# State space layer of a decoder: norm, D term and copies on ScalarE, the dt chain on operands in PSUM, the update of x two turns behind its power

## The chip, the cores and the metric

One core of a Trainium2 chip runs the whole kernel in one launch. The metric is the device time of one execution in microseconds (us), as the median of several runs. Engines are named as in the profile: PE (TensorE matmul; PEld its weight loads), DVE (VectorE), ACT (ScalarE), POOL (GpSimd), SP (SyncE, which issues DMAs). PSUM is the memory that PE writes, SBUF the other one on the chip.

## The reference

A decoder of two layers on x of 64 sequences x 128 positions x 256 features, all in float32. It has six blocks, each added to x: a state space layer (Mamba-like), cross attention, a recurrence, self attention, a wide cross attention, and a mixture of experts. Only the first block is touched by the change:

```
x = x + ssm(_layernorm(x))

zxbcdt = einsum('bld,ed->ble', x, in_proj_w)          # z 512, xBC 768, dt 8
xBC = silu(causal_conv4(xBC) + conv_b)                # x_part 512, B 128, C 128
dt = softplus(dt + dt_bias);  A = -exp(A_log)         # 8 heads
step:  decay = exp(A * dt_t)
       state = state * decay + (x_t * dt_t) outer B_t
       y_t = einsum('bhpn,bn->bhp', state, C_t)
y = y + x_part * D_full
y = y * silu(z)
y = y * rsqrt(mean(y*y) + EPS) * norm_w
return einsum('ble,de->bld', y, out_proj_w)
```

The kernel computes the scan over 128 positions as matrix products: with dA the product of dt and A, exp of its segment sums (`seg`) times B C^T (`gm`) is a 128x128 matrix `m` for each head, and y is `m` times `xdt` (x times dt).

## The kernel before

x stays in SBUF all the time, in 16 tiles `X[g]` of a group of four sequences (128 positions on the partitions, 4 x 256). The state space layer runs over the 16 groups and, in each, over four sequences; other blocks follow, one after the other, with tiles of their own.

Two generators write the layer. `mamba_inputs(g)` (L353) does a group: the norm (`norm`, L168: statistics on DVE, the root as a power on POOL at L165, then four subtract-and-multiply instructions on DVE, L191), the transposition of the normalised x on PE with a copy of one half on ACT (L204) and one on DVE (L206), then from the transposed x eight values dt a position (`pd`, L386), six convolutions (`conv`, L365) and four gates (`gate`, L379). A convolution is a projection on PE into one bank of PSUM, a scaled copy on ACT (L369), three multiply-adds on DVE (L373), a tanh on ACT (L362, which overwrites the projection's bank) and a last product on DVE (L363), which leaves `xc` in SBUF; a gate is a projection, a tanh and a product (`zs`). dt is softplus, written as max(v, 0) plus a series for log(1 + exp(-|v|)) (L390 to L407), 19 small instructions on DVE on tiles of 128x32 in SBUF, and one Exp on ACT (L392).

`mamba(g, b)` (L424) does a sequence: `ua` on POOL (L432), pg, px and seg on PE, an Exp over 128x1024 on ACT (L452), `m` on DVE (L455), py on PE (L461), the D term as four multiply-adds of 128x128 on DVE (L466), the gate and the sum of squares on POOL and ACT (L469 to L474), the output projection po (L479, with the sum of squares at L483), and the last three: ms on DVE (L488), its power on POOL (L165, `rs`), and the update of x on DVE (L490).

PSUM: the tag "mm" has six banks, which projections, pd, px, pg, py, po and the transposes take in turn; `seg` has the other two. A bank goes back when its last reader is done.

What sets the order: `run` (L49) gives each generator that is active one step a turn, from yield to yield; group g starts at turn 8g, sequence i at turn 2i + 8. This order is a priority only. A scheduler then fixes the order of each engine's queue when the kernel is built, and each engine works its queue strictly in that order, waiting on semaphores. SP's queue has in this stage the loads of x and weights and, once a sequence, a DMA that clears 1 MB of a scratch buffer (`clear`, L342), which nothing in the layer reads.

Of the kernel before, what the change touches and what calls it, by code (L numbers as in the profile page):

```python
# [7 lines left out]
F32 = mybir.dt.float32  # L8
I32 = mybir.dt.int32
AF = mybir.ActivationFunctionType  # L10
ALU = mybir.AluOpType
# [4 lines left out]
P = 128  # L16
D = 256
G = 4
T = G * P
LN_EPS = 1e-5  # L20
# [17 lines left out]
def mid(ap, n):  # L38

    return ap.unsqueeze(1).to_broadcast([ap.shape[0], n, ap.shape[1]])  # L40
# [22 lines left out]
def tile_decoder(ctx: ExitStack, tc: tile.TileContext, a: dict, out: bass.AP):  # L63
# [48 lines left out]
    X = []  # L112
# [83 lines left out]
    def transposed(work, ps, xn, bufs=2):  # L196

        xnT = [work.tile([P, T], F32, tag=f"xnT{c}", name=f"xnT{c}", bufs=bufs) for c in range(2)]
        for c in range(2):
            pt = ps.tile([P, T], F32, tag="mm", name="pt_ln")  # L200
            for b in range(G):
                nc.tensor.transpose(pt[:, b * P:(b + 1) * P], xn[:, b, c * P:(c + 1) * P], ident)  # L202
            if c == 0:
                nc.scalar.copy(xnT[c], pt)  # L204
            else:
                nc.vector.tensor_copy(xnT[c], pt)  # L206
        return xnT
# [143 lines left out]
    nc.gpsimd.tensor_scalar_mul(dpar, dpar, 0.5)  # L351

    def mamba_inputs(g, work, ps, got):  # L353
        xn = norm(work, g)
        yield
        xnT = transposed(work, ps, xn)
        yield

        def silu2(dst, u, th=None):
            if th is None:  # L360
                th = work.tile([P, T], F32, tag="th", name="th", bufs=2)
            nc.scalar.activation(th, u, AF.Tanh, scale=0.5)  # L362
            nc.vector.scalar_tensor_tensor(dst, th, 1.0, u, ALU.add, ALU.mult)  # L363

        def conv(c):  # L365
            pc = project(ps, win, 512 + c * P, P, xnT)
            acc = work.tile([P, G, P], F32, tag="acc", name="acc", bufs=2)
            pv = pc.rearrange("p (b t) -> p b t", b=G)
            nc.scalar.activation(  # L369
                acc, pv, AF.Identity, bias=convb[:, c:c + 1], scale=convw[:, c, 3:4]  # L370
            )
            for k in range(1, 4):
                nc.vector.scalar_tensor_tensor(  # L373
                    acc[:, :, k:], pv[:, :, :P - k], convw[:, c, 3 - k:4 - k], acc[:, :, k:],
                    ALU.mult, ALU.add,
                )
            silu2(xc[:, c, :], acc.rearrange("p b t -> p (b t)"), pc)

        def gate(c):  # L379
            silu2(zs[:, c, :], project(ps, win, c * P, P, xnT))  # L380


        pd = ps.tile([P, T], F32, tag="mm", name="pd")
        pdv = pd[:, :G * 8].rearrange("p (b h) -> p b h", b=G)
        for b in range(G):
            project_rows(pdv[:, b, :], xnT, win, b, slice(1280, 1288))  # L386
        v, u, r, s2, q, dt, da = (
            work.tile([P, G, 8], F32, tag=f"dt_{i}", name=f"dt_{i}", bufs=2) for i in range(7)
        )
        nc.vector.tensor_tensor(v, pdv, mid(dtb, G), ALU.add)  # L390
        nc.vector.scalar_tensor_tensor(u, v, -1.0, v, ALU.mult, ALU.max)
        nc.scalar.activation(u, u, AF.Exp, scale=-1.0)  # L392
        xc = work.tile([P, 6, T], F32, tag="xc", name="xc", bufs=2)
        conv(4)
        yield
        nc.vector.tensor_scalar(r, u, 2.0, None, ALU.add)
        nc.vector.reciprocal(r, r)
        nc.vector.tensor_tensor(u, u, r, ALU.mult)
        nc.vector.tensor_tensor(s2, u, u, ALU.mult)
        nc.vector.tensor_scalar(q, s2, 1.0 / 17, None, ALU.mult)  # L400
        for n in (15, 13, 11, 9, 7, 5, 3):
            nc.vector.scalar_tensor_tensor(q, q, 1.0 / n, s2, ALU.add, ALU.mult)
        nc.vector.scalar_tensor_tensor(q, q, 1.0, u, ALU.add, ALU.mult)
        nc.vector.tensor_scalar(v, v, 0.0, None, ALU.max)
        nc.vector.scalar_tensor_tensor(dt, q, 2.0, v, ALU.mult, ALU.add)
        nc.vector.tensor_tensor(da, dt, mid(negA, G), ALU.mult)  # L406
        nc.vector.tensor_scalar(dt, dt, 0.5, None, ALU.mult)  # L407
        conv(5)
        yield
        conv(0)  # L410
        conv(1)
        yield
        conv(2)
        zs = work.tile([P, 4, T], F32, tag="zs", name="zs", bufs=2)
        gate(0)
        yield
        conv(3)
        gate(1)
        yield
        gate(2)  # L420
        gate(3)
        got[g] = xc, zs, dt, da

    def mamba(g, b, work, ps, got):  # L424
        xc, zs, dt, da = got[g]
        clear(g * G + b)
        if g * G + b == B - 1:
            clear(B)
        tb = slice(b * P, (b + 1) * P)

        ua = work.tile([P, 8, P], F32, tag="ua", name="ua", bufs=2)
        nc.gpsimd.tensor_tensor(out=ua, in0=mid(upper, 8), in1=last(da[:, b, :], P), op=ALU.mult)  # L432

        pg = ps.tile([P, T], F32, tag="mm", name="pg")
        nc.tensor.matmul(pg[:, :P], lhsT=xc[:, 4, tb], rhs=xc[:, 5, tb], start=True, stop=True)
        gm = work.tile([P, P], F32, tag="gm", name="gm", bufs=2)
        nc.vector.scalar_tensor_tensor(gm, pg[:, :P], 0.25, upper, ALU.mult, ALU.mult)
        px = ps.tile([P, T], F32, tag="mm", name="px")
        for j in range(4):
            nc.tensor.transpose(px[:, j * P:(j + 1) * P], xc[:, j, tb], ident)  # L440
        xdt = work.tile([P, 8, 64], F32, tag="xdt", name="xdt", bufs=3)
        nc.vector.tensor_tensor(
            xdt, px.rearrange("p (h e) -> p h e", h=8), last(dt[:, b, :], 64), ALU.mult
        )
        yield
        seg = ps.tile([P, 8, P], F32, tag="seg", name="seg")
        for hf in range(2):
            nc.tensor.matmul(
                seg[:, hf * 4:hf * 4 + 4, :], lhsT=lower, rhs=ua[:, hf * 4:hf * 4 + 4, :],
                start=True, stop=True,  # L450
            )
        nc.scalar.activation(seg, seg, AF.Exp)  # L452
        yield
        m = work.tile([P, 8, P], F32, tag="m", name="m", bufs=3)
        nc.vector.tensor_tensor(m, seg, mid(gm, 8), ALU.mult)  # L455
        yield
        yield
        py = ps.tile([P, 4, P], F32, tag="mm", name="py")
        for h in range(8):
            r0 = (h % 2) * 64  # L460
            nc.tensor.matmul(  # L461
                py[r0:r0 + 64, h // 2, :], lhsT=xdt[:, h, :], rhs=m[:, h, :], start=True, stop=True
            )
        y = work.tile([P, 4, P], F32, tag="y", name="y", bufs=2)
        for j in range(4):
            nc.vector.scalar_tensor_tensor(  # L466
                y[:, j, :], xc[:, j, tb], dpar[:, j:j + 1], py[:, j, :], ALU.mult, ALU.add
            )
        nc.gpsimd.tensor_tensor(out=y, in0=y, in1=zs[:, :, tb], op=ALU.mult)  # L469
        ysq = work.tile([P, 4, P], F32, tag="ysq", name="ysq")  # L470
        nc.scalar.activation(ysq, y, AF.Square)
        nc.gpsimd.tensor_tensor(out=ysq[:, 0:2], in0=ysq[:, 0:2], in1=ysq[:, 2:4], op=ALU.add)
        sq = work.tile([P, P], F32, tag="sq", name="sq", bufs=3)
        nc.gpsimd.tensor_tensor(out=sq, in0=ysq[:, 0], in1=ysq[:, 1], op=ALU.add)  # L474
        yield
        yield
        po = ps.tile([P, T], F32, tag="mm", name="po")
        for j in range(4):
            nc.tensor.matmul(  # L479
                po[:, :D], lhsT=y[:, j, :], rhs=wout[:, j, :], start=(j == 0), stop=(j == 3)  # L480
            )
        yield
        nc.tensor.matmul(  # L483
            po[:, D:D + 1], lhsT=sq, rhs=ones[:, 0:1], start=True, stop=True
        )

        ms = work.tile([P, 1], F32, tag="ms", name="ms", bufs=2)
        nc.vector.tensor_scalar(ms, po[:, D:D + 1], 1.0 / 512, 4 * LN_EPS, ALU.mult, ALU.add)  # L488
        rs = power(work, "rs", ms)
        nc.vector.scalar_tensor_tensor(  # L490
            X[g][:, b, :], po[:, :D], rs, X[g][:, b, :], ALU.mult, ALU.add
        )

    with phase_pool("work1", "left") as work, phase_pool("ps1", space=PSUM) as psp:
        ps = PsumPool(psp, {"mm": 6, "seg": 1})
        got = {}
        run(
            [(8 * g, mamba_inputs(g, work, ps, got)) for g in range(NG)]
            + [(2 * i + 8, mamba(i // G, i % G, work, ps, got)) for i in range(B)]
        )  # L500
    w1_cm.__exit__(None, None, None)

# [740 lines left out]
```

## Time and profile before

| what | us |
|---|---|
| median of three runs | 3499.11 (3480.84 to 3499.29) |
| profiled execution, its own time | 3451.55 |
| its span, first to last instruction | 3449.8 |
| of it the state space layer, up to the last update of x | 789 |

The profiled execution is one run, some 1.4% below the median of the others. Inside the first 789 us the engines are busy so:

```profile
0.00:789.00 789.00, 711.03 (x3328) 425.20 (x3328) 683.22 (x1555) 280.42 (x418) 337.64 (x351) 0.97 0.32 105
789.00:1811.00 1022.00, 983.53 (x6174) 614.16 (x6174) 572.31 (x1204) 595.62 (x2387) 353.90 (x301) 0.99 0.05 17
```

A line gives the stretch and its length, then the busy time of PE, PEld, DVE, ACT and POOL with the number of instructions, the mean granted clock of PE (1 is full), the mean share of the DMA engines and GB/s. The second line is what follows, mainly cross attention and the recurrence. A line of instructions, as the prediction shows them, has the source line, engine, operation, the tiles written and read, the count, then busy us and mean ns of one, then the idle time of the engine just before them and what ended it.

### The profile page before, as it was taken

What the parts mean: (1) busy time and instruction counts of PE and PEld (TensorE: products, weight loads), DVE (VectorE), ACT (ScalarE), POOL (GpSimd) and SP (SyncE); (2) the same over time, 40 slices, a digit from 0 to 9 for tenths busy, and PEclk for the clock granted to TensorE, in tenths of its full rate; (3) what the DMA queues carried; (4) which work ended last, traced back from release to release, by engine and by line L of the source; (5) the groups of instructions that cost most, each with busy time, mean ns of one, the idle gap of its engine ahead of it and who ended that gap; (6) DMA issues with size and microseconds to landing.
All of it is one profiled execution on the core that took longest, in us unless ns stands there. A gap on an engine that the chain in (4) does not pass through costs nothing. (4 is left out here: it accounts for less than half of the span.)

```text
span 3449.8 us, 51423 instructions
## 1 busy us (share of the span) xinstructions
PE 3186.7 (92%) x17998; PEld 2011.8 (58%) x17998; DVE 2211.8 (64%) x5354; ACT 1627.1 (47%) x5829; POOL 1237.1 (36%) x1156
## 2 busy tenths in 40 slices
PE   7899899997999999999999788999999999689989
PEld 4555555554566666666656544555656565468845
DVE  7989899974555565556554375676676767543355
ACT  3333333333655565556655255565656666213300
POOL 3444344446233223332231055232322222223277
PEclk9999999998999999999999888998999999789999
DMA  9980000001000000000000111010101111157655
GB/s 313 343 290 1 1 1 1 1 14 30 13 13 13 25 13 13 13 24 14 13 13 13 34 44 56 30 45 25 44 32 41 35 39 36 62 175 228 201 183 178
DMA packets 172978, 229.65 MB, mean 67 GB/s; under 512 B 19760, under 2 KB 143152, under 8 KB 172720
## 3 DMA queue, kind: packets, MB, share of 16 engines
q1 hardware_dynamic: 154752, 180.19, 16.2%
q0 software_dynamic: 17968, 46.18, 4.3%
q8 instruction: 142, 2.33, 0.3%
q14 instruction: 116, 0.95, 0.1%
HBM read 113.71 MB, written 127.93 MB: 70 GB/s over the span
## 5 line engine op out<-in xcount | busy, mean ns | idle before, releaser
L267 ACT ACTIVATE e<-s,mx 128x128 f32<-128x128 f32 x2048 | 721.1, 378 | 398.2 <-DVE mx L256 247.4
L333 POOL TENSOR_TENSOR kbd<-kT,consts 128x512 f32<-128x512 f32 x192 | 201.6, 1050 | 863.2 <-PE s L247 861.9
L267 ACT ACTIVATION_READ_ACCUMULATOR e<-s,mx 128x1 f32 x2048 | 444.8, 217 | 0.0
L247 PE MATMUL s<-kbd,qT 64*128 64x512 f32 x1024 | 369.5, 657 | 5.4 <-ACT e L267 3.8
L216 PE MATMUL proj<-xnT,win 128*128 128x512 f32 x640 | 312.8, 629 | 48.5 <-DVE xc L363 45.0
L278 PE MATMUL pt<-consts,e 128*128 128x128 f32 x2048 | 326.7, 286 | 25.0 <-ACT e L267 18.6
L278 PEld LDWEIGHTS pt<-consts,e 128*128 128x128 f32 x2048 | 235.9, 143 | 131.8 <-ACT e L267 65.2
L282 DVE COPY eT<-pt 128x512 f32<-128x512 f32 x256 | 175.6, 686 | 157.1 <-PE pt L278 155.2
L216 PEld LDWEIGHTS proj<-xnT,win 128*128 128x128 f32 x640 | 121.7, 200 | 195.2 <-issue 117.2
L873 POOL DMA_INDIRECT xs<-xnr,r_rows x128 | 125.5, 981 | 269.7 <-DMA xs<-xnr,r_rows 188.4
L373 DVE SCALAR_TENSOR_TENSOR acc<-proj,convw,acc 128x508 f32<-128x508 f32 (+2 forms) x288 | 209.5, 731 | 9.5 <-ACT acc L369 7.9
L632 PE MATMUL pu<-c,fu 128*128 128x128 f32 x1536 | 188.3, 281 | 14.9 <-DVE c L647 14.9
L309 PE MATMUL av<-eT,v 128*32 128x128 f32 x4096 | 181.5, 284 | 17.9 <-DVE oT L318 12.8
L632 PEld LDWEIGHTS pu<-c,fu 128*128 128x128 f32 x1536 | 182.6, 196 | 21.9 <-PE pv L224 13.6
L165 POOL TENSOR_TENSOR ln_rstd<-ln_ve,neghalf 128x4 f32<-128x4 f32 x96 | 97.9, 1019 | 271.1 <-DVE ln_ve L178 249.8
L252 DVE TENSOR_REDUCE mx<-s 128x4 f32<-128x512 f32 x256 | 170.1, 677 | 29.0 <-PE s L247 28.5
L432 POOL TENSOR_TENSOR ua<-consts,dt 128x1024 f32<-128x1024 f32 x64 | 121.9, 1905 | 178.3 <-DVE dt L406 150.4
L216 PE MATMUL proj<-xnT,fx 128*128 128x512 f32 x384 | 175.0, 605 | 0.5 <-ACT xnT L204 0.5
L280 ACT COPY eT<-pt 128x512 f32<-128x512 f32 x256 | 154.4, 603 | 39.9 <-PE pt L278 35.3
L309 PEld LDWEIGHTS av<-eT,v 128*32 128x32 f32 x4096 | 102.3, 110 | 118.3 <-issue 56.6
L256 DVE TENSOR_REDUCE mx<-s 128x8 f32<-128x1024 f32 x128 | 155.9, 1218 | 22.0 <-PE s L247 21.9
L191 DVE TENSOR_SCALAR xn<-x,ln_mv,ln_rstd 128x256 f32<-128x256 f32 x256 | 129.8, 552 | 37.2 <-POOL ln_rstd L165 37.2
(269 smaller groups left out, 6460.7 us busy)
## 6 DMA issues: line engine op xcount, KB each, us to landing
xs<-zeros SPq DMA_DIRECT2D x64, 1024.0 KB, 11.2
xs<-xs SPq DMA_DIRECT2D x71, 256.0 KB, 3.4
ys<-y SPq DMA_DIRECT2D x71, 256.0 KB, 2.3
ctxT<-in_ctxT_dram SPq DMA_DIRECT2D x32, 512.0 KB, 3.8
xo<-xo SPq DMA_DIRECT2D x32, 512.0 KB, 3.5
x<-in_x_dram SPq DMA_DIRECT2D x16, 512.0 KB, 8.9
xn<-xnT SPq DMA_DIRECT2D x32, 256.0 KB, 2.0
xnT<-xn SPq DMA_DIRECT2D x16, 512.0 KB, 4.3
```

Of the source, the lines that this page charges most:

```text
L216: nc.tensor.matmul(o[:m, :], lhsT=w[:, k, m0:m0 + m], rhs=rhs[k], start=(k == 0), stop=(k == 1))
L247: nc.tensor.matmul(ss[hf], lhsT=q[rows], rhs=kb[rows, :, :], start=True, stop=True)
L252: nc.vector.tensor_reduce(mxs[i], ss[i], AX.X, ALU.min)
L256: nc.vector.tensor_reduce(mx, s, AX.X, ALU.min)
L267: nc.scalar.activation(e[h // 4][:, h % 4, :], sh[h], AF.Exp, bias=mh[h], scale=-1.0, accum_out=den[:, c * 8 + h:c * 8 + h + 1],)
L278: nc.tensor.transpose(pt[:, h, :], e[i][:, h, :], ident)
L280: nc.scalar.copy(eT[i], pt)
L282: nc.vector.tensor_copy(eT[i], pt)
L309: nc.tensor.matmul(av[j * 32:j * 32 + 32, c, :], lhsT=vh(h), rhs=eT[h // 4][:, h % 4, :], start=(odd == 0), stop=(odd == 1),)
L333: nc.gpsimd.tensor_tensor(out=kb, in0=mid(k, 4), in1=last(head, P), op=ALU.mult)
L373: nc.vector.scalar_tensor_tensor(acc[:, :, k:], pv[:, :, :P - k], convw[:, c, 3 - k:4 - k], acc[:, :, k:], ALU.mult, ALU.add,)
L632: nc.tensor.matmul(pu[:, i, :], lhsT=fu[:, k, c * P:(c + 1) * P], rhs=c2[:, k, :], start=(k == 0), stop=(k == 1),)
```

## The change

Seven edits, all in the state space layer:

1. The norm is written out in `mamba_inputs`. DVE computes only an offset, -mean x rstd, for the four sequences at once; ACT applies scale and offset. The norm and its use are one step apart.
2. Both copies of the transposed x are on ACT.
3. The dt chain keeps v, u, z, s2 and dt2 in the unused columns of pd's PSUM bank instead of SBUF tiles, so that most of its instructions have one operand in PSUM and one in SBUF. The absolute value and the square are on ACT (Abs, Square), the series is scaled so that two instructions go.
4. The D term: ACT multiplies x by D into a new tile `xd` one step after the sequence starts; DVE adds it to py in one instruction of 128x512.
5. `m` has two buffers instead of three.
6. The update of x stands two yields behind the power that it needs.
7. The steps of the convolutions and gates are cut elsewhere, and the sequences start at turn 2i + 9.

```diff
     def mamba_inputs(g, work, ps, got):
-        xn = norm(work, g)
-        yield
-        xnT = transposed(work, ps, xn)
+        x = X[g]
...
+        rstd = power(work, "ln_rstd", ve)
+        yield
+
+        off = work.tile([P, G], F32, tag="ln_off", name="ln_off", bufs=2)
+        nc.vector.scalar_tensor_tensor(off, mv[:, :, 0], -1.0, rstd, ALU.mult, ALU.mult)
+        xn = work.tile([P, G, D], F32, tag="xn", name="xn")
+        for b in range(G):
+            nc.scalar.activation(
+                xn[:, b, :], x[:, b, :], AF.Identity, bias=off[:, b:b + 1], scale=rstd[:, b:b + 1]
+            )
+        yield
...
+            nc.scalar.copy(xnT[c], pt)
         yield
...
-        pdv = pd[:, :G * 8].rearrange("p (b h) -> p b h", b=G)
+        pdv, v, u, z, s2, dt2 = (
+            pd[:, i * 32:(i + 1) * 32].rearrange("p (b h) -> p b h", b=G) for i in range(6)
+        )
...
-        v, u, r, s2, q, dt, da = (
-            work.tile([P, G, 8], F32, tag=f"dt_{i}", name=f"dt_{i}", bufs=2) for i in range(7)
+        r, q, dt, da = (
+            work.tile([P, G, 8], F32, tag=f"dt_{i}", name=f"dt_{i}", bufs=2) for i in range(4)
         )
         nc.vector.tensor_tensor(v, pdv, mid(dtb, G), ALU.add)
-        nc.vector.scalar_tensor_tensor(u, v, -1.0, v, ALU.mult, ALU.max)
+        nc.scalar.activation(u, v, AF.Abs)
         nc.scalar.activation(u, u, AF.Exp, scale=-1.0)
...
-        nc.vector.tensor_scalar(r, u, 2.0, None, ALU.add)
+        nc.vector.tensor_scalar(r, u, 0.5, 1.0, ALU.mult, ALU.add)
         nc.vector.reciprocal(r, r)
-        nc.vector.tensor_tensor(u, u, r, ALU.mult)
-        nc.vector.tensor_tensor(s2, u, u, ALU.mult)
+        nc.vector.tensor_tensor(z, u, r, ALU.mult)
+        nc.scalar.activation(s2, z, AF.Square, scale=0.5)
+        conv(5)
+        yield
         nc.vector.tensor_scalar(q, s2, 1.0 / 17, None, ALU.mult)
         for n in (15, 13, 11, 9, 7, 5, 3):
             nc.vector.scalar_tensor_tensor(q, q, 1.0 / n, s2, ALU.add, ALU.mult)
-        nc.vector.scalar_tensor_tensor(q, q, 1.0, u, ALU.add, ALU.mult)
-        nc.vector.tensor_scalar(v, v, 0.0, None, ALU.max)
-        nc.vector.scalar_tensor_tensor(dt, q, 2.0, v, ALU.mult, ALU.add)
-        nc.vector.tensor_tensor(da, dt, mid(negA, G), ALU.mult)
-        nc.vector.tensor_scalar(dt, dt, 0.5, None, ALU.mult)
-        conv(5)
-        yield
+        nc.vector.scalar_tensor_tensor(q, q, 1.0, z, ALU.add, ALU.mult)
+        nc.vector.scalar_tensor_tensor(dt2, v, 0.0, q, ALU.max, ALU.add)
+        nc.vector.tensor_tensor(da, dt2, mid(negA, G), ALU.mult)
+        nc.vector.tensor_scalar(dt, dt2, 0.5, None, ALU.mult)
         conv(0)
...
         nc.scalar.activation(seg, seg, AF.Exp)
+
+        xd = work.tile([P, 4, P], F32, tag="xd", name="xd", bufs=2)
+        for j in range(4):
+            nc.scalar.mul(xd[:, j, :], xc[:, j, tb], dpar[:, j:j + 1])
         yield
-        m = work.tile([P, 8, P], F32, tag="m", name="m", bufs=3)
+        m = work.tile([P, 8, P], F32, tag="m", name="m", bufs=2)
...
-        for j in range(4):
-            nc.vector.scalar_tensor_tensor(
-                y[:, j, :], xc[:, j, tb], dpar[:, j:j + 1], py[:, j, :], ALU.mult, ALU.add
-            )
+        nc.vector.tensor_tensor(y, py, xd, ALU.add)
...
         rs = power(work, "rs", ms)
+        yield
+        yield
         nc.vector.scalar_tensor_tensor(
             X[g][:, b, :], po[:, :D], rs, X[g][:, b, :], ALU.mult, ALU.add
         )
...
-            + [(2 * i + 8, mamba(i // G, i % G, work, ps, got)) for i in range(B)]
+            + [(2 * i + 9, mamba(i // G, i % G, work, ps, got)) for i in range(B)]
```

The built order of the blocks behind the layer is the same on PE, DVE, ACT and POOL in both programs.

More of the change, by code (lines that the diff above doesn't have):

```diff
@@ L353, in mamba_inputs @@
     def mamba_inputs(g, work, ps, got):
-        xn = norm(work, g)
-        yield
-        xnT = transposed(work, ps, xn)
+        x = X[g]
+        st = work.tile([P, G, 6], F32, tag="ln_st", name="ln_st", bufs=2)
+        mv = work.tile([P, G, 2], F32, tag="ln_mv", name="ln_mv", bufs=2)
+        for b in range(G):
+            nc.vector.bn_stats(st[:, b, :], x[:, b, :])
+        for b in range(G):
+            nc.vector.bn_aggr(mv[:, b, :], st[:, b, :])
+        ve = work.tile([P, G], F32, tag="ln_ve", name="ln_ve", bufs=2)
+        nc.vector.tensor_scalar(ve, mv[:, :, 1], LN_EPS, None, ALU.add)
+        rstd = power(work, "ln_rstd", ve)
+        yield
+        off = work.tile([P, G], F32, tag="ln_off", name="ln_off", bufs=2)
+        nc.vector.scalar_tensor_tensor(off, mv[:, :, 0], -1.0, rstd, ALU.mult, ALU.mult)
+        xn = work.tile([P, G, D], F32, tag="xn", name="xn")
+        for b in range(G):
+            nc.scalar.activation(
+                xn[:, b, :], x[:, b, :], AF.Identity, bias=off[:, b:b + 1], scale=rstd[:, b:b + 1]
+            )
+        yield
+        xnT = [work.tile([P, T], F32, tag=f"xnT{c}", name=f"xnT{c}", bufs=2) for c in range(2)]
+        for c in range(2):
+            pt = ps.tile([P, T], F32, tag="mm", name="pt_ln")
+            for b in range(G):
+                nc.tensor.transpose(pt[:, b * P:(b + 1) * P], xn[:, b, c * P:(c + 1) * P], ident)
+            nc.scalar.copy(xnT[c], pt)
         yield
@@ L402, in mamba_inputs @@
             nc.vector.scalar_tensor_tensor(q, q, 1.0 / n, s2, ALU.add, ALU.mult)
-        nc.vector.scalar_tensor_tensor(q, q, 1.0, u, ALU.add, ALU.mult)
-        nc.vector.tensor_scalar(v, v, 0.0, None, ALU.max)
-        nc.vector.scalar_tensor_tensor(dt, q, 2.0, v, ALU.mult, ALU.add)
-        nc.vector.tensor_tensor(da, dt, mid(negA, G), ALU.mult)
-        nc.vector.tensor_scalar(dt, dt, 0.5, None, ALU.mult)
-        conv(5)
+        nc.vector.scalar_tensor_tensor(q, q, 1.0, z, ALU.add, ALU.mult)
+        nc.vector.scalar_tensor_tensor(dt2, v, 0.0, q, ALU.max, ALU.add)
+        nc.vector.tensor_tensor(da, dt2, mid(negA, G), ALU.mult)
+        nc.vector.tensor_scalar(dt, dt2, 0.5, None, ALU.mult)
+        conv(0)
         yield
-        conv(0)
         conv(1)
+        conv(2)
         yield
-        conv(2)
         zs = work.tile([P, 4, T], F32, tag="zs", name="zs", bufs=2)
         gate(0)
+        conv(3)
         yield
-        conv(3)
         gate(1)
-        yield
         gate(2)
```

## The prediction

> **What bounds the kernel now.** I read the page's slices first, then windows, groups by shape, waits and one timeline, all inside the stage that the change touches.
>
> ```profile
> PE   7899899997999999999999788999999999689989
> DVE  7989899974555565556554375676676767543355
> ...
> 550.00:650.00 100.00, 91.71 (x434) 54.70 (x433) 91.63 (x197) 38.61 (x58) 44.50 (x47) 1.00 0.00 1
> ...
> L406 DVE TENSOR_TENSOR dt<-dt,negA x16: 175/180/185, 30.3 to 731.5; 128x32 f32<-128x32 f32 x16
> ```
>
> A slice is 86 us. Only in the first nine (the state space layer, last update of x at 789 us) is DVE as full as PE. In the window line (busy of PE, PEld, DVE, ACT, POOL, then the granted clock) both stand at 92%. L406 runs once per group of four sequences: 16 times, 30.3 to 731.5 us, so (731.5-30.3)/15 = 46.75 us per group. That period is what can change.
>
> ```profile
> L466 DVE SCALAR_TENSOR_TENSOR y<-xc,dpar,py 128x128 f32<-128x128 f32 x256 | 73.6, 337 | 8.1 <-PE py L461 8.1
> L191 DVE TENSOR_SCALAR xn<-x,ln_mv,ln_rstd 128x256 f32<-128x256 f32 x64 | 48.3, 802 | 3.1 <-POOL ln_rstd L165 3.1
> L490 DVE SCALAR_TENSOR_TENSOR x<-po,rs,x 128x256 f32<-128x256 f32 x62 | 29.9, 483 | 48.0 <-POOL rs L165 47.9
> L407 DVE TENSOR_SCALAR dt<-dt 128x32 f32<-128x32 f32 x16 | 23.7, 1481 | 0.0
> L402 DVE SCALAR_TENSOR_TENSOR dt<-dt,dt 128x32 f32<-128x32 f32 x112 | 19.8, 177 | 0.0
> L391 DVE SCALAR_TENSOR_TENSOR dt<-dt 128x32 f32<-128x32 f32 x16 | 15.4, 962 | 0.1
> ...
> L191 DVE TENSOR_SCALAR xn<-x,ln_mv,ln_rstd 128x256 f32<-128x256 f32 x64 | 25.1, 433 | 8.5 <-POOL ln_rstd L165 8.5
> ```
>
> Two things to see. The same L191 takes 802 ns in this stage (0 to 785 us) and 433 ns between 900 and 1500 us; L407 takes 1481 ns for 32 columns where L402 takes 177. And DVE stands 47.9/16 = 3.0 us per group waiting for POOL's power before L490. DVE is thus busy 91% and stopped by its own queue for 6% more: it sets the pace.
>
> ```profile
> PE proj L216 <- DVE xc L363: 45.0, 23, 4.8
> ...
> 362.51 9.67 PE L216 MATMUL proj<-xnT,win 128*128 128x512 f32 x16 [4.76 <-DVE xc L363]
> ...
> 412.74 5.39 PE L216 MATMUL proj<-xnT,win 128*128 128x512 f32 x12 [1.05 <-DVE y L466]
> 417.96 1.89 PE L479 MATMUL po<-wout,y 128*128 128x256 f32 x8
> 419.78 1.09 PE L461 MATMUL py<-m,xdt 128*64 128x128 f32 x16
> ```
>
> PE's waits from 60 to 740 us end on DVE: the bank of a convolution comes free only when DVE has written xc. After the idle 4.76 us, 16 projection records take 9.67 us; elsewhere 12 take 5.39, that is 0.43 each after a 0.6 us tail. So a long stop is paid twice.
>
> **PE's own need.** From such rows, start to start: proj 40 records x 0.43 = 17.2; seg 16 x 0.43 = 6.9; po 32 x 0.216 = 6.9; py 64 x 0.055 = 3.5; px, pd, pt_ln, pg 48 x 0.11 = 5.3; sums 0.5. Together 40.3 us a group, 6.4 below the period.
>
> **What the Trainium skill says.** "SBUF — State Buffer", section "Who interferes with whom": DVE and GpSimd share one port pair under an exclusive lock; a DVE tensor_scalar or copy in a two-port mode, or any DVE instruction with two SBUF inputs, can lose the whole length of a GpSimd instruction to it, and one with at most one SBUF input outside those modes does not. The trace agrees: L191 and L407 are stretched while POOL's 1.9 us L432 and 1.27 us L469 run beside them. "VectorE: DVE Perf Modes", "Why PSUM operands drop a tier": an fp32 operand in PSUM keeps an instruction out of the two-port mode; L373, with one operand in PSUM, holds 731 ns with no such spread. "ScalarE: Activation LUTs", "What ACT_TABLE_LOAD costs": 186 ns + 0.833 ns per element + 93 ns per pointer operand, 93 ns overlapped; L369 (two pointers, 512) would be 798 ns, the trace has 774. "TensorE: Matmul & The Clock Gate", "What's actually happening": idleness halves the clock; the 362 us line agrees.
>
> **The change, part by part (per group, before its period is recomputed).**
> Norm: four L191, 4 x 802 = 3.2 us, leave DVE; one tiny instruction for the offset (0.2) comes, -3.0. ACT gains 4 x about 0.49 = 2.0 (price above, two pointers, 256 columns, less overlap). The second transposed copy (L206, 0.68) goes from DVE to ACT (0.59).
> dt chain: L391 (0.96), L399 (0.42) and L404 (0.23) go; ACT gains Abs and Square at L392's 0.22 each. L407 1.48, L400 0.60, L398 0.43 should fall to about 0.18 as L402: -2.0. With the three removed, -3.6. The trace has no operation wholly in PSUM of this size but L390 (pd in, 180 ns), so between 0.18 and 0.25 each; I take 0.18, the ends differ by 1 us of DVE, which isn't the bound then.
> D term: 16 L466 become 4 additions of 128x512. L442 (PSUM in, 128x512) costs 0.68. Four L466 in a row take 1.11 us in the timeline, so 4 x 0.43 = -1.7. ACT gains 16 multiplications, 386 - 93 = 0.29 each, 4.7 us.
> So DVE: 91% of 46 = 41.9, less 3.0 + 0.7 + 3.6 + 1.7 and about 0.5 given back for overlaps, is 33.4 us. ACT: 38% of 46 = 17.4, plus 2.0 + 0.6 + 0.4 + 4.7 is 25. POOL stays about 20. PE, 40.3, is the next bound; DVE's relief is worth at most 6.4 us a group.
> Update of x: in the built order, DVE has 28, 2, 3 and 0 instructions between the power's input (ms) and the update for the four sequences of a group (before 0 or 1, 1, 2 and 1). The first three waits go; the fourth stays, 0.55 us of power and handovers, but in DVE's slack.
> What is added: the update that stands 28 instructions later keeps its po bank some 13 us longer (sum of the rows between), and pd keeps a bank until dt is done, some 15 us instead of 1. Of six banks, four remain in that stretch. m goes from three buffers to two; its readers stand one turn behind, no wait is seen for it. ACT's queue gets x-scaled copies ahead of the convolution's first instruction; behind them stand acc and tanh, for which DVE waits.
> Start one turn later: the order of all engines behind this stage is the same in both programs, and inside it the built order, not the turn, decides; I count nothing. The 64 clearing DMAs, issued at each sequence's start, stand in SP's queue in the same order as before, behind nothing new.
>
> **A walk through one steady group**, with the built order and the durations above, from the first pd (t = 0). PE: pd 1.8, conv4 3.5, pg and px, conv5 6.0, seg 7.7, po 9.4, conv0 11.1, py 12.0, seg and pg 14.05. px then needs py's bank, free when DVE has added y: DVE's queue gets conv4's acc at 5.0, xc at 9.0, m at 11.65, conv5's xc 12.3, conv0's three acc (one after ACT, 12.1) 14.5, y 15.25. PE idles 1.3 us, then 0.8 more for conv0's xc (ACT's exp stands ahead of its tanh). From 16.6 on PE finds its banks: conv1, conv2, gate0, conv3 23.5, po 25.2, three gates 32.8, po 35.4, py 36.3, transposes 38, seg, po, py: 42.3, and the next pd can start. Stalls 2.1 us; none long enough to halve the clock.
> With some of the jitter that a walk hides I take 42.9. Saving (46.75-42.9) x 15 = 58 us. Filling and draining: the norm's two more handovers against a shorter chain, nothing. The profiled run of before took 3451.6 us (span 3449.8 and 1.8 around it): 3394 by its own scale. The median of the three runs is 3499.1, 1.4% above it; the stage's saving carried there gives 3441.
>
> **Rivals.**
> *PE's bound alone:* DVE's slack hides the two waits, 41.4 us a group: -80, 3419. For it: PE is busy 97.7% from 900 to 1500 us; against it: the px wait follows from the order.
> *Banks come back as waits:* in the stretch of 20 us with four banks, twelve tiles pass; a convolution holds its bank at least 1.9 + 0.8 + 2.2 + 0.6 + 0.7 = 6.2 us. If holds average 2 us above the walk's, 45 us a group: -26, 3473. For it: PE waits on xc already; against: DVE has 20% slack.
> *Slower:* the same place, one step further: the held po and pd banks let PE stop for more than about 4 us once a group, so that each stop also halves the clock (the 362 us line: 4.76 idle and 9.67 instead of 7.0 after it, 7.5 us in all). 40.3 + 1 + 7.5 = 48.8 a group, +31, 3530. It decides once y at L494 comes 3 us later than walked, for instance through ACT's longer queue; the walk has ACT 59% busy there.
> *The offload doesn't shorten anything* because contention, not the operands, makes the long rows: 46.7, no change. Against: L402 and L373.
>
> **Chances.** Walk 0.62 (own range 3425 to 3458), PE's bound 0.12, banks 0.17, slower 0.05, no change 0.04. Range 3400 to 3482: both faster rivals inside. A measurement tells 0.5%, 17 us, from nothing. Faster: walk, PE's bound and nearly all of the banks case, 0.90; same 0.05; slower 0.05.
>
> **What would show it.** Group period near 43 and the layer's end near 730 us; DVE busy about 78% and PE 96% of a steady window; the dt rows near 180 ns whatever POOL does; one short wait before the fourth update; PE's largest wait at px, not on xc; granted clock 1.00 throughout. A period above 45 with waits on banks of po or pd would make it wrong; long rows for the PSUM chain too.

## The result and the profile after

The changed kernel takes 3437.93 us (median of four runs, 3435.68 to 3440.68), the kernel before 3492.2 us in the runs beside it. The ratio is 0.9843, 95% interval 0.9822 to 0.9865: 54 us saved, 47 to 62 by the interval. Forecast were 3441 us and 58 us saved.

The groups of the layer follow each other at these times; first the slices of the changed kernel's span on its page (40 of equal length, busy share in tenths):

```profile
PE   7999999989999999999999688999999998699778
DVE  7888777755565555655554456767677776433344
```

Then the line that runs once a group, and the update of x, from the views of these two lines (count, ns of one as least, median and most, then the start of the first and of the last in us):

```profile
L433 DVE TENSOR_TENSOR dt<-pd,negA x16: 182/184/186, 32.4 to 686.1; 128x32 f32<-128x32 f32 x16
```

```profile
L518 DVE SCALAR_TENSOR_TENSOR x<-po,rs,x x64: 476/483/485, 86.0 to 739.6; 128x256 f32<-128x256 f32 x64
```

In the slices of the layer PE is now full and DVE mostly at seven or eight tenths; before, both were nearly full. The group takes (686.1 - 32.4)/15 = 43.58 us instead of 46.75, and the layer ends (its last update of x starts) at 739.6 us instead of 789.0, 49.4 us earlier. This is the saving; the built order of everything behind it is unchanged.

The windows of the changed kernel (length, then busy PE, PEld, DVE, ACT, POOL, then the granted clock):

```profile
350.00:450.00 100.00, 96.65 (x505) 60.68 (x504) 77.72 (x174) 57.22 (x116) 48.59 (x51) 1.00 0.00 1
450.00:550.00 100.00, 96.65 (x463) 58.00 (x461) 78.55 (x166) 54.10 (x107) 44.07 (x46) 0.98 0.00 1
```

PE stands at nearly 97% and DVE at 78%, where both were between 89 and 92% before. The rows on DVE (whole layer: busy us, mean ns, idle time before them and its releaser):

```profile
L518 DVE SCALAR_TENSOR_TENSOR x<-po,rs,x 128x256 f32<-128x256 f32 x64 | 30.8, 482 | 29.4 <-POOL rs L165 28.8
L430 DVE SCALAR_TENSOR_TENSOR dt<-dt,pd 128x32 f32<-128x32 f32 x112 | 20.0, 179 | 0.0
L367 DVE SCALAR_TENSOR_TENSOR ln_off<-ln_mv,ln_rstd 128x4 f32<-128x4 f32 x16 | 14.7, 916 | 3.1 <-POOL ln_rstd L165 3.1
L434 DVE TENSOR_SCALAR dt<-pd 128x32 f32<-128x32 f32 x16 | 3.0, 185 | 0.0
```

L434, the old L407, takes 185 ns instead of 1481. Its input is in PSUM now, but its place in the order has changed too; the run with the chain in SBUF, below, tells the two apart. The new L367 has both its inputs in SBUF and takes 916 ns for four columns: twelve of the 16 run while POOL works and take 1168 ns on average, the four others 160. The wait for POOL's power before the update of x has shrunk over the whole layer from 50.5 to 28.8 us (the prediction's 47.9 leaves out the last two updates), less than hoped. On PE, one group of the changed kernel (start us, us, engine, what, count; in brackets the idle time before it and its releaser):

```profile
401.49 1.95 PE L224 MATMUL pd<-win,xnT 128*128 128x8 f32 x16
...
412.95 1.09 PE L490 MATMUL py<-m,xdt 128*64 128x128 f32 x16
413.98 0.38 PE L509 MATMUL po<-consts,sq 128*128 128x1 f32 x2
...
417.15 0.66 PE L465 MATMUL px<-consts,xc 128*128 128x128 f32 x4 [0.75 <-DVE y L494]
418.74 7.13 PE L216 MATMUL proj<-xnT,win 128*128 128x512 f32 x16 [0.93 <-DVE xc L386]
425.71 1.89 PE L505 MATMUL po<-wout,y 128*128 128x256 f32 x8
427.53 1.09 PE L490 MATMUL py<-m,xdt 128*64 128x128 f32 x16
428.55 0.49 PE L460 MATMUL pg<-xc 128*128 128x128 f32 x2
428.88 0.60 PE L465 MATMUL px<-consts,xc 128*128 128x128 f32 x4
...
445.62 0.61 PE L224 MATMUL pd<-win,xnT 128*128 128x8 f32 x4
```

From pd to pd 44.13 us. PE stops twice and briefly, at the two places and for the two releasers that the walk had: px behind y, the next projection behind xc. After the stops 16 projection records take 7.13 us, full speed; the stop of 4.76 us with its slow records is gone. One of the later groups differs, and takes 45.83 us:

```profile
507.00 8.83 PE L216 MATMUL proj<-xnT,win 128*128 128x512 f32 x16 [1.10 <-DVE xc L386]
```

Its two stops are no longer in sum, 0.58 and 1.10 us, but behind them the clock granted from 506 to 510 us is 0.66.

The two profiled executions differ by 16 us only, 3451.55 and 3435.68, since another block differs against the change: from the last update in the wide attention to the end, the experts took 447 us in the profile of before (2998.0 to 3445.4) and 496 in that of the changed kernel (2933.8 to 3429.6). Both lengths occur with either version of the layer, as the last section shows.

### The profile page after: what moved, and what is told of

Same layout as the page of the kernel before. It is cut to its first block, busy times and chain, and to the rows that moved or that the text cites. A ratio compares the mean times of both kernels' runs of the same rounds, so it can differ in the third digit from the quotient of the medians.

```text
span 3433.9 us, 51466 instructions
## 1 busy us (share of the span) xinstructions
PE 3167.8 (92%) x17998; PEld 2005.7 (58%) x17998; DVE 2096.1 (61%) x5050; ACT 1745.8 (51%) x6197; POOL 1235.6 (36%) x1156
## 5 line engine op out<-in xcount | busy, mean ns | idle before, releaser
L216 PE MATMUL proj<-xnT,win 128*128 128x512 f32 x640 | 298.5, 610 | 16.3 <-DVE xc L386 16.3
L495 POOL TENSOR_TENSOR y<-y,zs 128x512 f32<-128x512 f32 x64 | 81.3, 1271 | 230.3 <-DVE y L494 222.5
L1103 POOL DMA_INDIRECT ys<-ys,t_yrow x128 | 122.4, 957 | 93.6 <-DVE x L1115 44.6
```

The lines of the kernel that those rows point to most:

```text
L216: nc.tensor.matmul(o[:m, :], lhsT=w[:, k, m0:m0 + m], rhs=rhs[k], start=(k == 0), stop=(k == 1))
```

## The experiments

Two theories were open. The prediction's: DVE set the pace, and PE does now. Its rival: the pace is made by waits between the engines, over banks above all, and relief of DVE is only one way to shorten them. All ratios are to the kernel before on the same chip, with 95% intervals; the layer's end is that of the one profiled execution (before 789.0, changed 739.6).

**Extra work on one engine.** In both kernels, DVE's multiplication into xdt, or the matmuls of one projection in each group, are done twice; the result is the same.

```diff
-        nc.vector.tensor_tensor(
-            xdt, px.rearrange("p (h e) -> p h e", h=8), last(dt[:, b, :], 64), ALU.mult
-        )
+        for _ in range(2):
+            nc.vector.tensor_tensor(
+                xdt, px.rearrange("p (h e) -> p h e", h=8), last(dt[:, b, :], 64), ALU.mult
+            )
```

```diff
-            silu2(zs[:, c, :], project(ps, win, c * P, P, xnT))
+            pz = project(ps, win, c * P, P, xnT)
+            for k in range(2 if c == 0 else 0):
+                nc.tensor.matmul(
+                    pz, lhsT=win[:, k, c * P:(c + 1) * P], rhs=xnT[k], start=(k == 0), stop=(k == 1)
+                )
+            silu2(zs[:, c, :], pz)
```

> The kernel before, with the 128x512 product xdt on DVE written twice (four more DVE instructions of 0.68 us a group, about 2.5 us without overlaps). Theory (DVE sets the pace before): the group period grows by 2.0 to 2.7 us, the time by 30 to 40 us against before. Rival (the pace is set by waits between engines, not by DVE's work): less than half of that, under 18 us.

> The kernel before, with the first gate's projection written twice (four more PE records of 0.43 us a group, 1.7 us). Theory (PE has 6 us a group to spare before): 0 to 8 us more than before. Rival (PE and DVE are equally the bound): 20 to 27 us more.

> The changed kernel with xdt written twice, 2.5 us of DVE a group. Theory (DVE has slack now): 0 to 10 us more than the changed kernel, so 44 to 54 us below before. Rival (DVE still paces, through the waits of PE on its banks): 30 us or more above the changed kernel, so 25 us or less below before.

> The changed kernel with the first gate's projection written twice, 1.7 us of PE a group. Theory (PE sets the pace now): 24 to 28 us more than the changed kernel, period 44.1 to 45.8, about 28 us below before. Rival (the 3.8 us a group above PE's own need are waits on other engines, which the extra work fills): under 13 us more.

| run | ratio | interval | layer's end, us |
|---|---|---|---|
| before, DVE twice | 1.0225 | 1.0169 to 1.0280 | 878.4 |
| before, PE twice | 1.0041 | 1.0027 to 1.0055 | 800.7 |
| changed, DVE twice | 0.9873 | 0.9823 to 0.9924 | 741.5 |
| changed, PE twice | 0.9966 | 0.9949 to 0.9983 | 778.2 |

The same DVE work costs 79 us in the kernel before and some 10 us in the changed one (0.9873 against 0.9843, intervals overlapping; its layer ends 1.9 us later). The same PE work costs 14 us before and 43 us after. So the bound did move from DVE to PE, as forecast, though before PE wasn't quite free either (0 to 8 us were expected). Two sizes are off. The DVE work of 40 us before cost twice that; one window of that run, and the waits of its PE (what waits, for whom; us, count, longest us), show where the time goes:

```profile
450.00:550.00 100.00, 88.99 (x411) 53.54 (x409) 82.32 (x182) 31.74 (x48) 38.05 (x41) 0.93 0.00 1
```

```profile
PE proj L216 <- DVE xc L363: 52.2, 26, 2.7
PE pt_ln L202 <- DVE xn L191: 36.2, 12, 3.5
```

The clock granted there is 0.93, where the kernel before has 0.98 in the same stretch, and PE has got a second long wait, for the norm on DVE. A kernel that starves PE pays for the idle time and, as far as this window shows, for the lower clock after it. DVE itself is busy only 82% there, where it has 91% in this stretch of the kernel before. So DVE's work alone doesn't make that pace: about half of the loss is waiting between the engines, as the rival says, and the rival is not excluded for it. The changed kernel with PE's work doubled lost 43 us where 27 were expected. Eight of its 15 intervals between groups are 45.81 to 45.85 us, the 44.13 and the 1.72 added, but six are 47.06 or 47.55, with a granted clock of 0.96 or 0.97. Two places of it show the difference (the same records behind stops of about the same size, slow and fast):

```profile
438.14 7.12 PE L216 MATMUL proj<-xnT,win 128*128 128x512 f32 x12 [0.94 <-DVE xc L386]
485.69 5.42 PE L216 MATMUL proj<-xnT,win 128*128 128x512 f32 x12 [1.10 <-DVE xc L386]
```

That is 1.7 us in six groups, some 10 of the 16 us. Why the clock falls in these groups and not in the others, with stops of the same size, and where the rest lies, is open; the scheduler also built another order.

**One part alone**, on the kernel before: edits 1 and 2, edit 3, edits 4 and 5, edit 6, each as in the diff of the change, the rest as before.

> The kernel before with edits 1 and 2 alone (norm and both copies on ACT). DVE loses 3.0 + 0.7 us a group by the prediction, less 0.7 for the offset, which took 0.92 us in the changed kernel. Theory (before, time follows DVE's work until PE's 43 to 44 us a group): 35 to 48 us less than before, nearly as much as the whole change. Rival (each part brings its share of the 54 us, the parts add up): 15 to 20 us less.

> The kernel before with edit 3 alone (dt chain on operands in PSUM, Abs and Square on ACT). DVE loses about 3.6 us a group. Theory: 35 to 48 us less than before. Rival (parts add up): 15 to 20 us less. If pd's bank, held for the whole chain, is what PE lacks: no gain or slower.

> The kernel before with edits 4 and 5 alone (D term on ACT, m with two buffers). DVE loses 1.7 us a group, ACT gains 16 multiplications of 0.3 us. Theory: 20 to 30 us less than before. Rival (parts add up): 8 to 12 us less.

> The kernel before with edit 6 alone (update of x two yields later). Theory: DVE's 3.0 us a group of waiting for POOL's power falls to 1 to 1.5, so 20 to 30 us less than before. Rival 1 (parts add up): 8 to 12 us less. Rival 2 (po's bank held longer costs PE what DVE gains): within 8 us of before.

| run | ratio | interval | layer's end, us | DVE's wait for the power, us |
|---|---|---|---|---|
| norm and copies | 0.9932 | 0.9908 to 0.9957 | 765.6 | 75.0 |
| dt chain | 0.9881 | 0.9852 to 0.9910 | 749.6 | 48.4 |
| D term | 0.9933 | 0.9911 to 0.9955 | 774.2 | 29.4 |
| late update | 1.0027 | 1.0011 to 1.0043 | 795.9 | 35.8 |

The dt chain alone brings 1.2%, three quarters of the whole. The D term brings 23 us, as the theory had it. The norm brings 23 us where 35 to 48 were expected: part of what it frees on DVE goes into a wait, shown in its profile:

```profile
L513 DVE SCALAR_TENSOR_TENSOR x<-po,rs,x 128x256 f32<-128x256 f32 x64 | 30.8, 482 | 75.0 <-POOL rs L165 75.0
...
L430 DVE TENSOR_SCALAR dt<-dt 128x32 f32<-128x32 f32 x16 | 5.3, 333 | 0.0
```

75.0 us of waiting for the power, against 50.5 before. The second line is the last instruction of the dt chain, still in SBUF here, at 333 ns instead of 1481: four of the 16 run while POOL works and take 788 ns on average, the other twelve 182. So one edit, which changes what POOL runs beside a row, changes the rows of another. The late update alone makes the kernel slower, where 20 to 30 us less were expected: it takes 15 us of DVE's waits away and ends the layer 7 us later. The three gains add up to 0.68 + 1.19 + 0.67 = 2.5%, more than the 1.6% of all edits together, and still 2.3% less the late update's loss. So they overlap, or one edit costs more beside the others than alone. Edit 7, the new cut of the steps, was not run alone; what it brings or costs is open.

**The change without one of its parts.** First without edit 6; then with the eight banks of PSUM in one pool (seg in two tiles of one bank, Exp and m by halves); then both; last with the dt chain's operands in SBUF, while Abs and Square stay on ACT.

```diff
         rs = power(work, "rs", ms)
-        yield
-        yield
```

```diff
-        seg = ps.tile([P, 8, P], F32, tag="seg", name="seg")
+        segs = [ps.tile([P, 4, P], F32, tag="mm", name="seg") for _ in range(2)]
...
-        ps = PsumPool(psp, {"mm": 6, "seg": 1})
+        ps = PsumPool(psp, {"mm": 8})
```

```diff
-        pdv, v, u, z, s2, dt2 = (
-            pd[:, i * 32:(i + 1) * 32].rearrange("p (b h) -> p b h", b=G) for i in range(6)
-        )
+        pdv = pd[:, :32].rearrange("p (b h) -> p b h", b=G)
...
-        r, q, dt, da = (
-            work.tile([P, G, 8], F32, tag=f"dt_{i}", name=f"dt_{i}", bufs=2) for i in range(4)
+        r, q, dt, da, v, u, z, s2, dt2 = (
+            work.tile([P, G, 8], F32, tag=f"dt_{i}", name=f"dt_{i}", bufs=2) for i in range(9)
         )
```

> The changed kernel without edit 6 (update of x right behind its power). Theory (after s4_late: a bank held longer costs PE as much as DVE gains): within 5 us of the changed kernel, or up to 15 us faster, period 43.2 to 44.3; DVE's waits for the power rise. Rival (the prediction's: DVE's waits matter): 8 us or more slower than the changed kernel.

> The changed kernel with all eight banks of PSUM in one pool: seg is two tiles of one bank, Exp and m go by halves. Theory (PE's stops of 0.8 and 1.2 us a group before px and the next projection are waits for a bank): 15 to 30 us faster than the changed kernel, period about 42.3, the two waits gone. Rival (those stops stand for late work of DVE that something else will wait for, or the halves cost more): within 6 us or slower.

> Eight banks and no late update, together. Theory: the better of the two or a little better than both, 15 to 35 us faster than the changed kernel. Rival: as a_nolate alone.

> The changed kernel with v, u, z, s2 and dt2 in SBUF tiles instead of pd's bank; Abs and Square stay on ACT. Theory (the long rows come from the port that DVE and POOL share): some of the chain's rows rise from 0.18 to 0.4 to 1.5 us, DVE gets 2 to 3 us a group more, and as DVE has slack the time grows by 3 to 15 us. Rival (the length was not the operands' place, but the two instructions that went to ACT): rows stay at 0.18, time within 3 us.

| run | ratio | interval | layer's end, us |
|---|---|---|---|
| the change (first comparison) | 0.9843 | 0.9822 to 0.9865 | 739.6 |
| without the late update | 0.9797 | 0.9769 to 0.9824 | 720.5 |
| eight banks | 0.9866 | 0.9840 to 0.9892 | 745.4 |
| eight banks, no late update | 0.9791 | 0.9766 to 0.9816 | 717.9 |
| dt chain in SBUF | 0.9786 | 0.9762 to 0.9810 | 711.0 |

Without the late update the layer ends 19 us earlier. Its loss shows also between the two kernels with eight banks, which ran side by side: 3395.17 us with it (3388.99 to 3399.55), 3369.55 without (3362.52 to 3376.74). And it doesn't even spare DVE its waits, which were expected to rise without it; this is the update of x without edit 6, where the changed kernel waits 28.8 us:

```profile
L516 DVE SCALAR_TENSOR_TENSOR x<-po,rs,x 128x256 f32<-128x256 f32 x64 | 30.8, 481 | 24.5 <-POOL rs L165 24.5
```

With the dt chain back in SBUF the layer ends 28.6 us earlier. That kernel has the lowest ratio, 0.9786, though its interval overlaps those of the two kernels without the late update. Two of its windows, and then rows of the dt chain on DVE:

```profile
450.00:550.00 100.00, 99.09 (x494) 61.06 (x493) 84.54 (x165) 56.12 (x111) 45.67 (x48) 1.00 0.00 1
550.00:650.00 100.00, 99.16 (x498) 62.09 (x497) 78.67 (x157) 57.45 (x117) 48.14 (x51) 1.00 0.00 1
```

```profile
L428 DVE SCALAR_TENSOR_TENSOR dt<-dt,dt 128x32 f32<-128x32 f32 x112 | 31.0, 277 | 0.0
L426 DVE TENSOR_SCALAR dt<-dt 128x32 f32<-128x32 f32 x16 | 10.5, 655 | 0.0
L429 DVE SCALAR_TENSOR_TENSOR dt<-dt,dt 128x32 f32<-128x32 f32 x16 | 6.3, 394 | 0.0
L432 DVE TENSOR_SCALAR dt<-dt 128x32 f32<-128x32 f32 x16 | 2.7, 169 | 0.0
```

Some rows did rise, 179 to 277 ns in the series, 182 to 655 at its start, as the theory of the shared port says. In the series, 37 of the 112 run while POOL works and take 481 ns on average, the others 176; with an operand in PSUM, 23 run beside POOL and take 179, the others 178.

The last row, L432, didn't rise, though it is the old L407 with its input in SBUF again. The timelines show why, first before, then here:

```profile
409.56 0.18 DVE L406 TENSOR_TENSOR dt<-dt,negA 128x32 f32<-128x32 f32 x1
409.66 0.73 DVE L373 SCALAR_TENSOR_TENSOR acc<-proj,convw,acc 128x500 f32<-128x500 f32 x1
409.89 1.90 POOL L432 TENSOR_TENSOR ua<-consts,dt 128x1024 f32<-128x1024 f32 x1 [9.60 <-DVE dt L406]
410.31 1.51 DVE L407 TENSOR_SCALAR dt<-dt 128x32 f32<-128x32 f32 x1
```

```profile
405.12 0.17 DVE L431 TENSOR_TENSOR dt<-dt,negA 128x32 f32<-128x32 f32 x1
405.22 0.17 DVE L432 TENSOR_SCALAR dt<-dt 128x32 f32<-128x32 f32 x1
405.44 1.90 POOL L455 TENSOR_TENSOR ua<-consts,dt 128x1024 f32<-128x1024 f32 x1 [0.27 <-DVE dt L432]
```

Before, another instruction stands between L406 and L407, and POOL's ua, which L406 releases, is at work when L407 comes: so in 15 of 16 groups, with 1502 to 1897 ns for L407. Here, as in the changed kernel, the last row follows at once and is done before ua has run for 20 ns. For this row the order is enough; PSUM wasn't needed. By the sums of their rows, the chain takes 105.7 us of DVE before, 49.6 in the changed kernel and 73.2 here: of the 56 us that left DVE, 24 came back with the operands in SBUF.

DVE is busier, 83% instead of 78% between 250 and 650 us. But PE is busy 99%, and its waits before px have gone, all but one of 1.8 us between 60 and 700 us. DVE had the slack to pay for that, PE had none. So the theory was right about part of the rows and wrong about the sign: the chain in pd's bank saves DVE time that isn't needed any more, and PE stops more where it is there.

The reason looks like the bank held for the length of the chain, and in edit 6 the bank of po. But eight banks in one pool didn't help (0.9866, where 15 to 30 us less than the changed kernel were expected), and without the late update they made no clear difference either (0.9791 against 0.9797). The stop only moved. In the first of these runs PE waits before a projection for y:

```profile
PE proj L216 <- DVE y L494: 17.9, 9, 2.1
```

This is 2 us, once a group, where px had stood before. All eight banks are in use in either layout, only shared otherwise, and each run has an order of its own from the scheduler. What is shown is that taking either of the two long holds away brings some 15 to 20 us by the ratios (for the late update the intervals touch, but the pair with eight banks agrees); that the bank itself is the cause, and not the order that comes with it, is not shown. The two removals together were not run.

## Why the prediction was right, and where not

Time and direction: 3441 us against 3437.93, a saving of 58 against 54. The mechanism holds in the main: the bound moved from DVE to PE, shown by the work added to one engine at a time. That the total came so near is in part luck: errors of both signs cancelled, and in the two profiled executions the layer ends only 49.4 us earlier.

The walk: it had PE stop for 1.3 us before px, on y, and 0.8 us before the next projection, on xc. The trace has 0.75 and 0.93 us idle at those places with those releasers, and no long stop. DVE's share (78%) and PE's (96%) are as forecast, the dt rows stand at 178 to 200 ns (the reciprocal, which didn't change, at 344), and the clock is 0.98 to 1.00. That no stop is long enough to lower the clock held in all steady groups but one, where it cost 1.7 us. Two signs came out otherwise: PE's larger wait is on xc, not at px (9.2 against 5.8 us between 250 and 650 us), and DVE waits for the power about twice a group (17 times in those nine groups), not once.

The mis-sized term is PE's own need. The prediction put it at 40.3 us a group, from intervals inside a run of equal records. The group above takes 44.13 us with 1.7 us of stops, that is 42.4. The groups with the dt chain in SBUF agree: PE is busy 99% there, and the steady ones take 42.0 to 42.8 us. What was left out is where one tile's records end and the next one's begin. Each py takes 1.02 or 1.03 us from its start to the start of the next tile (412.95 to 413.98) instead of the 0.88 that its records sum to; po takes up to 1.82 (425.71 to 427.53) instead of 1.73, pg up to 0.33 (428.55 to 428.88) instead of 0.22. That makes a steady group 1.2 us longer than the 42.9 taken, some 18 us in 15 groups. About half of it was given back by the start of the layer: the first interval between groups is 34.77 us, where it was 42.80 before, so the mean of all 15 is 43.58. The prediction counted filling at nothing.

The norm: its offset was put at 0.2 us, L367 took 0.92. The rule on two SBUF inputs (the Trainium skill, "SBUF — State Buffer", section "Who interferes with whom"), which the prediction quoted for other rows, covers this one too, and was not applied to it; the 1168 ns beside POOL and 160 without agree with it. DVE has slack in the changed kernel, so no loss of time from it is seen.

The late update: the step said that three of four waits go and that the fourth lies in DVE's slack; its longer hold of po's bank was not priced as a cost of this edit. The waits fell from 50.5 to 28.8 us only, and without the edit they are 24.5. The edit is a loss: 9 us on the kernel before, some 16 in the changed one (0.9843 against 0.9797, intervals that touch; 19 us in the layer's end). The rival "banks come back as waits" named a place for such a loss, with 0.17; the walk contained its size, 2.1 us a group. The prediction treated those stops as part of the best case and didn't ask which edit brings them.

The dt chain: right in size, 56 us of DVE less over 16 groups, or 3.5 a group where 3.6 were forecast, and worth 41 us on the kernel before, where DVE is the bound. For its longest row the reason was only half right: L407 was stretched by POOL's ua, but another place in the order frees it without PSUM. Of the removals tried, that of the placement in PSUM ends the layer earliest. The slower rival, with stops above 4 us, didn't occur.

## What to carry to other kernels

In this kernel, relief of the bounding engine paid only up to the next bound, and what came with it (a bank held longer, a later release, another order) was paid by that next engine: after the bound has moved, try each edit's removal again. Find the bound by writing one instruction of an engine twice, and price the next bound with the handovers between tiles, not only within a run of equal instructions. A row that is far longer than its neighbour of the same size, as L407 with 1481 ns beside L402 with 177, can be looked up in the timeline for what runs beside it; here another place in the order was enough. Making it short is a gain only on the engine that sets the pace.

## What was not expected of the hardware

The block of experts at the end takes two lengths. In the profile of before it is 447 us, in that of the changed kernel 496; in the first four experiments, beside which the kernel before had a median of 3496.57 us, it is 494 to 497 in all four kernels, and in the other eight, beside medians of 3442.32 and 3436.96 us, 448 to 451. The code of the block is the same in all of them, and its built order the same in the kernels before and changed; each of the three sets of experiments was on a chip of its own. So times are compared through the kernel before, run beside each set. The cause wasn't looked for.

A small instruction can cost as much as the POOL instruction beside it: L407, 128x32, took 1502 to 1897 ns beside the 1.9 us of ua, and its counterpart in SBUF 169 ns when it stood just ahead of ua.

Short stops can be enough for a lower clock: behind stops of 0.58 and 1.10 us, with px between them, 16 projection records took 8.83 us once in the changed kernel, where 7.13 is usual.

Added work on DVE came back doubled here: some 40 us of it cost 79, with a granted clock of 0.93 instead of 0.98 in the middle of the layer.
